# Linear attention gated by a Hadamard FFN: the second pair's transform by matrix products, a chained layernorm and a divided elu step

## The chip, the cores and the metric

The kernel runs on one core of one Trainium2 chip, and everything is computed in 32-bit floats. The metric is the device time of one execution in microseconds (us). Three runs before the change took 1621.09, 1618.7 and 1622.43 us, with a median of 1621.09 us.

## The reference, cut to what matters

The input x holds eight sequences of 512 tokens with 512 features. Every token is normalized, and the result `xn` goes two ways: into a linear attention `s`, and into a gated FFN `g` whose weights stand behind Walsh-Hadamard transforms (`fwht`). The output is `x + s * g`.

```python
xn = _layernorm(x)
q, k, v = xn @ Wq.T + bq, xn @ Wk.T + bk, xn @ Wv.T + bv
context = (elu(q) + 1) * cumsum((elu(k) + 1) * v, axis=1) * 32 ** -0.5
s = context @ Wo.T + bo
h = fwht(xn * SU_ug) / 64
up, gate = h @ W_up.T * (Ws_up * 64), h @ W_gate.T * (Ws_gate * 64)
ffn = (fwht(silu(gate) * up * SU_dp) / 64) @ W_down.T * (Wscale_dp * 64)
out = x + s * silu(ffn)
```

A transform over 512 features can be done as butterflies in nine levels of additions and subtractions, or as products with a 128x128 Hadamard matrix for seven of the levels and butterflies for the other two.

## The kernel before, in words

**Pairs.** The eight sequences are worked in four pairs, p = 0 to 3, sequences 2p and 2p+1 together. In each pair come six projections (k, v, q for two halves of the heads; `attention`, L777), then four hidden units u = 0 to 3, of which u = 0 is followed by the output projection (`project_out`, L846), and u = 1 and u = 3 by a half of the down projection (`down`, L950). In the first pair the weights are loaded raw, encoded on VectorE (`first_w`, `hidden_w`, L1010) and stored to DRAM. Later pairs stream the encoded weights back. A hidden unit of the first pair is two `gate` and two `up` groups; in later pairs it is one `hidden_unit` (L892) of seven block products.

**Products.** All products use a seven-product scheme: operands are held as seven factors P1 to P7, three or four of them sums and differences that VectorE or GpSimd makes (`outer_factors`, `inner_tokens`, `encode_tokens`, `encode_weights`). A `group` (L535) runs seven products of one projection. ScalarE copies the partial sum out of PSUM three times (`sa`, `sb`, `sc`: `snapshot`), VectorE adds the two other accumulators (`output`, L560), and the PSUM bank of `px` goes on to the next product only when the snapshot is taken.

**Order.** The program is traced by a planner. `at(place, fn)` puts a step into an agenda at a number of places ahead; one place is one product of the group. A group advances it by 14 places, a hidden unit by 49, the output projection by 28, half a down projection by 56 or a little more. The steps of a group overlap those of the next: its last products lie at places 18 and 22. `later(us, fn)` puts VectorE work into a queue that `pace` empties: behind each output, as many items as make up the given number of us, and at least one. `catch_up` empties the queue at once. `background` gives what is traced in it a priority 150 steps lower. The trace is then put into an order for each engine by priority and by what is expected to be ready, so an instruction can come well ahead of its place. Once built, each engine takes its own instructions in that order; SyncE (SP) issues nearly all DMAs.

**The tokens of the next pair.** `normalized(b)` (L179) loads sequence b, normalizes it on VectorE (statistics L202, scale L212), stores it (`put("x")`, L198), multiplies it by `su` on GpSimd (L222) and stores that too (`put("xs")`). `transformed(b)` (L244) loads this back and does nine levels of butterflies in two instructions each on VectorE (L255), then stores the result (`d_xh`). `hidden_tokens` (L297) loads it again turned around by `squares` (L262, in pieces of 128 bytes) and transposes it on VectorE (`turned`); `next_tokens` (L284) does the same with the untransformed tokens for the attention. For the first pair the transform is done differently, by `first_transform` (L348) in the attention: products with `hads`, the Hadamard matrix scaled by the signs, pinned in TensorE's program order, then two levels of butterflies.

**Where it all stands.** For the second pair (sequences 2 and 3) `normalized` is called behind groups 13 and 14 of the first pair, and `transforms(0)` behind group 16 (`plan`, L1209). For later pairs `normalized(2p + 2)` is called behind the attention, `normalized(2p + 3)` behind the output projection, and `transforms(p)` behind the second hidden unit. Tiles of sequences above 3 are in the pool `xin`, which has one buffer, shared with `squares`; the other large tiles are in `t8`, which has six.

**The rest that is touched.** `elu_plus_one` (L792) is traced as a whole behind the last product of a k or q group:

```python
for h in range(2):
    nc.scalar.activation(neg[:, h], r[:, h], AF.Relu, scale=-1.0)
    nc.scalar.activation(neg[:, h], neg[:, h], AF.Exp, scale=-1.0)
    nc.vector.scalar_tensor_tensor(r[:, h], r[:, h], 1.0, neg[:, h], ALU.add, ALU.max)
```

`chain_down` (L1194) folds the Hadamard transform into the down weights in four blocks during the first pair: ten VectorE instructions of 128x1024 each (L1036, L1041), and then four pinned products `pwd` (L1055, `fold_down`) 10 places behind them.

Of the kernel before, what the change touches and what calls it, by code (L numbers as in the profile page):

```python
# [8 lines left out]
F32 = mybir.dt.float32  # L9
# [12 lines left out]
def kernel(  # L22
# [156 lines left out]
    def normalized(b, delay=12):  # L179


        if b > 3:
            t = xin.tile([P, 3, 7, P], F32, tag="x", name=f"x_{b}").rearrange("p c s e -> p (c s e)")
            xt = t[:, : NT * D].rearrange("p (n d) -> p n d", n=NT)
            su = t[:, NT * D : (NT + 1) * D]
        else:
            xt = t8.tile([P, NT, D], F32, tag="t", name=f"x_{b}")
            su = hads
# [26 lines left out]

        def store():
            put("x")
            at(10, times_scales)

        def times_scales():  # L220
            for t in range(NT):
                nc.gpsimd.tensor_tensor(xt[:, t], xt[:, t], su, ALU.mult)  # L222
            put("xs")

        def start():
            if b > 3:
                with background():
                    for t in range(NT):
                        stats(t)
                    root()  # L230
                    for t in range(NT):
                        scaled(t)
                    store()
                return
            for t in range(NT):
                later(0.8, stats, t)
            later(0.3, root)
            for t in range(NT):
                later(0.6, scaled, t)
            later(0.0, store)  # L240

        at(delay, start)
# [19 lines left out]
    def squares(name, pool):  # L262


        if pool is t8:
# [30 lines left out]

    def hidden_tokens(b, xp):  # L297

# [46 lines left out]
        if s == 1:  # L345
            nc.vector.tensor_tensor(xo[:, P4], xo[:, P2], xo[:, P6], ALU.subtract)

    def first_transform(s, xa, xp):  # L348

        t = t8.tile([P, KD, L], F32, tag="t", name=f"xh_{s}")  # L350

        def product(c):
            x = (xa[:, (P1, P2)[c // 2]] if s == 0 else (xp[:, P7], xa[:, P3])[c // 2])[:, c % 2 : c % 2 + 3 : 2, :]
            p = ps.tile([P, 2, H], F32, tag="t", name=f"ph_{s}_{c}")
            tc.keep_in_program_order(
                nc.tensor.matmul(p, hads[:, c * P : (c + 1) * P], x, start=True, stop=True)
            )
            return p.rearrange("p a t -> p (a t)")

        def products(j):  # L360
            a, b = product(j), product(j + 2)
            nc.scalar.copy(t[:, j + 2], b)
            nc.vector.tensor_tensor(t[:, j], a, t[:, j + 2], ALU.add)
            nc.vector.tensor_tensor(t[:, j + 2], a, t[:, j + 2], ALU.subtract)

        def butterflies():
# [165 lines left out]
        return ps.tile([P, n, L // n], F32, tag=tag, bufs={"px": 3, "py": 1, "pz": 2, "t": 2}[tag], name=f"{tag}_{name}")  # L532


    def group(name, ws, rhs, dst, then, bias=(None, None)):  # L535

# [21 lines left out]
            return s  # L558

        def output(i, s, p):  # L560
            pace(nc.vector.tensor_tensor(dst[i], s, p.rearrange("p a t -> p (a t)"), ALU.add), 2.7)

        px, py, pz = (bank(t, name, 2) for t in ("px", "py", "pz"))
        sums = {}
# [212 lines left out]
    def attention(p, xo, co, get_w):  # L777
        def project(m, g, then):
# [4 lines left out]
            def whole(px):  # L783
# [8 lines left out]
        def elu_plus_one(r, name):  # L792
            neg = t8.tile([P, 2, 2, L], F32, tag="t", name=f"neg_{name}")
            for h in range(2):
                nc.scalar.activation(neg[:, h], r[:, h], AF.Relu, scale=-1.0)
                nc.scalar.activation(neg[:, h], neg[:, h], AF.Exp, scale=-1.0)
                nc.vector.scalar_tensor_tensor(r[:, h], r[:, h], 1.0, neg[:, h], ALU.add, ALU.max)

        def heads(g):
            phi = {}  # L800
# [13 lines left out]

            def with_q(q):
                k = phi["k"]
                elu_plus_one(q, f"q_{p}_{g}")
                for h in range(2):
# [3 lines left out]
                encode_tokens(nc.gpsimd, co[:, g])  # L822

            project("k", g, with_k)
            project("v", g, with_v)
# [184 lines left out]
    def hidden_w(name, src, f):  # L1010
# [13 lines left out]
    wd_f = dram.tile([FF, D], F32, tag="wd_f", name="wd_f")  # L1024

    def load_down(o):
        nc.sync.dma_start(rs[:, o % 2], wdown_t[:, o * P : (o + 1) * P].rearrange("(c p) e -> p c e", p=P))

    def butterflies_down(o, then):
# [155 lines left out]
    for c in range(KD):  # L1185
        nc.vector.tensor_scalar(hads[:, c * P : (c + 1) * P], had, col("su_ug", c), None, ALU.mult)
    groups = [0]

    def begin_down():
# [19 lines left out]
    plan = {  # L1209
        13: [lambda: normalized(2)], 14: [lambda: normalized(3)], 16: [lambda: transforms(0)],  # L1210
        0: [lambda: first_transform(0, xa, xp)], 1: [lambda: first_transform(1, xa, xp)], 2: [begin_down],
        3: [lambda: load_down(1)], 4: [lambda: nc.sync.dma_start(bo_r, bo.partition_broadcast(P))],
    }
    for n, u, j in ((16, 2, 0), (17, 2, 1), (18, 3, 0), (19, 3, 1)):
# [8 lines left out]
    def transforms(p):  # L1223

        even = transformed(2 * p + 2)
        if p:
            with background():
                for step in even[:8]:
                    step()
            even = even[8:]  # L1230
        for step in even:
            later(1.2, step)

        def odd():
# [5 lines left out]
    for p in range(B // 2):  # L1240
        more = p + 1 < B // 2
        if p:
            catch_up()
            xp = token_factors(f"xp_{p}")
            hidden_tokens(2 * p, xp)
            co = new_h(f"co_{p}")
        attention(p, xa, co, get_w)
        catch_up()
        if p and more:
            normalized(2 * p + 2)  # L1250
        hos = []
        for u in range(NU):
            if p == 0:
# [80 lines left out]
```

## Time and profile before

| what | value |
|---|---|
| median of three runs | 1621.09 us |
| the profiled execution | 1621.48 us |
| its span, first to last instruction | 1619.5 us |
| mean granted TensorE clock | 0.983 |
| TensorE busy, share of the span | 1535.8 us, 95% |
| VectorE busy | 1114.8 us, 69% |
| GpSimd busy | 479.5 us, 30% |
| ScalarE busy | 394.4 us, 24% |
| DMA, share of 16 engines | 59.1% |
| butterflies of the transforms (L255) on VectorE | 60 + 48 instructions, 77.7 + 59.1 us |

The profile names an engine (PE is TensorE, PEld its weight loads, DVE VectorE, ACT ScalarE, POOL GpSimd, SP SyncE), the line of the kernel and the tile written and read. "Idle before" is the time that an engine stood still ahead of an instruction, with what released it. A 32-bit product is two rows in the profile, one for each of two passes; passes of 512 columns follow each other every 0.43 us (four rows take 1.72 us from start to start), those of 256 columns every 0.216 us. Where the granted clock is halved, these intervals double. So one place of the planner is about 0.86 us.

### The profile page before, as it was taken

The numbers are of one execution on the slowest core, as the hardware profiler recorded it, in microseconds if no ns is written. First come the engines' busy times: TensorE is split into PE (matmuls) and PEld (weight loads), VectorE is DVE, ScalarE is ACT, GpSimd is POOL, SyncE is SP. The second block draws the span as 40 slices with busy tenths as digits, with TensorE's granted clock in tenths as the row PEclk, the third lists the DMA queues.
The fourth block names the chain that finished last, engine by engine and source line by source line (L and its number), as shares of the span: only waits on it lengthen the run. The fifth ranks groups of instructions, "written<-read, shape, count | busy, mean of one in ns | idle before, by whom it ended". The sixth has DMA issues, their size and how long they took to land. (4 is left out here: it accounts for less than half of the span.)

```text
span 1619.5 us, 15480 instructions
## 1 busy us (share of the span) xinstructions
PE 1535.8 (95%) x5792; PEld 1103.7 (68%) x5792; DVE 1114.8 (69%) x1470; ACT 394.4 (24%) x608; POOL 479.5 (30%) x270
## 2 busy tenths in 40 slices
PE   7989999897799989999999998999999999999998
PEld 3435547543484478888885476888887458888887
DVE  6999764499445984878673886598675596552673
ACT  4453221112014421111213431111211441111211
POOL 1122234142420064303611137120632026120631
PEclk9989999999899999999999999999999999999999
DMA  8347796866977256555586445737586624425462
GB/s 250 98 124 223 223 315 208 272 167 188 259 227 156 103 196 217 150 185 189 159 259 157 130 140 186 240 85 242 174 249 173 146 78 149 166 80 183 153 250 94
DMA packets 260602, 293.33 MB, mean 181 GB/s; under 512 B 107312, under 2 KB 209200, under 8 KB 256432
## 3 DMA queue, kind: packets, MB, share of 16 engines
q1 hardware_dynamic: 259856, 292.32, 59.1%
q8 instruction: 45, 0.74, 0.2%
q14 instruction: 29, 0.24, 0.0%
q10 hardware_dynamic: 672, 0.03, 0.0%
HBM read 203.72 MB, written 88.61 MB: 180 GB/s over the span
## 5 line engine op out<-in xcount | busy, mean ns | idle before, releaser
L621 PE MATMUL px_dn<-w_down,ho 128*128 128x256 f32 x1024 | 228.5, 379 | 0.0
L621 PEld LDWEIGHTS px_dn<-w_down,ho 128*128 128x128 f32 x1024 | 194.6, 190 | 28.2 <-issue 1.9
L723 PE MATMUL px_gu<-xi,w_gu 128*128 128x256 f32 x672 | 175.7, 384 | 5.0 <-DVE sb_gu L733 3.5
L723 PE MATMUL px_gu<-xp,w_gu 128*128 128x256 f32 x672 | 173.0, 380 | 1.3 <-DMA w_gu<-d_gu 1.3
L922 POOL TENSOR_TENSOR u<-u,v 128x1024 f32<-128x1024 f32 x24 | 56.1, 2360 | 350.2 <-DVE u L761 350.2
L723 PEld LDWEIGHTS px_gu<-xi,w_gu 128*128 128x128 f32 x672 | 127.3, 191 | 28.8 <-DVE sb_gu L733 4.3
L723 PEld LDWEIGHTS px_gu<-xp,w_gu 128*128 128x128 f32 x672 | 127.3, 190 | 21.0 <-DMA w_gu<-d_gu 2.0
L621 PE MATMUL pz_dn<-w_down,ho 128*128 128x256 f32 x496 | 112.9, 380 | 3.7 <-POOL ho L393 2.9
L621 PEld LDWEIGHTS pz_dn<-w_down,ho 128*128 128x128 f32 x496 | 93.5, 190 | 19.5 <-POOL ho L393 3.7
L723 PE MATMUL pz_gu<-xi,w_gu 128*128 128x256 f32 x336 | 86.6, 380 | 2.1 <-DVE a L754 1.1
L723 PE MATMUL pz_gu<-xp,w_gu 128*128 128x256 f32 x336 | 86.6, 380 | 1.1 <-DVE a L765 1.0
L967 POOL TENSOR_TENSOR s<-s,d 128x512 f32<-128x512 f32 x30 | 39.0, 1302 | 163.7 <-ACT d L966 124.6
L723 PE MATMUL py_gu<-xp,w_gu 128*128 128x256 f32 x336 | 87.4, 382 | 0.0
L390 POOL TENSOR_TENSOR co<-co 128x512 f32<-128x512 f32 x8 | 12.8, 1601 | 250.3 <-DVE co L819 250.3
L255 DVE TENSOR_TENSOR xh<-xs 128x1024 f32<-128x1024 f32 x60 | 77.7, 1325 | 7.6 <-DMA xs<-d_xs 7.2
L723 PEld LDWEIGHTS pz_gu<-xi,w_gu 128*128 128x128 f32 x336 | 63.4, 190 | 12.1 <-DVE u L754 2.0
L545 PE MATMUL px_gate<-xp,w_gate 128*128 128x512 f32 x128 | 62.7, 623 | 9.2 <-ACT sb_gate L555 9.2
L723 PEld LDWEIGHTS pz_gu<-xp,w_gu 128*128 128x128 f32 x336 | 63.7, 190 | 11.0 <-DVE a L765 2.4
L723 PEld LDWEIGHTS py_gu<-xp,w_gu 128*128 128x128 f32 x336 | 64.3, 192 | 9.3 <-DVE a L742 0.4
L621 PE MATMUL py_dn<-w_down,ho 128*128 128x256 f32 x256 | 60.4, 391 | 8.8 <-DMA w_down<-d_down 8.8
L545 PE MATMUL px_v<-xa,w_v 128*128 128x512 f32 x128 | 62.8, 611 | 6.0 <-ACT sc_v L557 6.0
L926 POOL TENSOR_TENSOR v<-v,r 128x1024 f32<-128x1024 f32 x24 | 57.4, 2410 | 24.3 <-DVE r L761 17.9
(264 smaller groups left out, 2744.6 us busy)
## 6 DMA issues: line engine op xcount, KB each, us to landing
w_gu<-d_gu SPq DMA_DIRECT2D x84, 896.0 KB, 4.5
w_down<-d_down SPq DMA_DIRECT2D x56, 512.0 KB, 3.8
d_s<-o SPq DMA_DIRECT2D x8, 1024.0 KB, 6.2
d_d<-dn SPq DMA_DIRECT2D x8, 1024.0 KB, 7.0
d<-d_d SPq DMA_DIRECT2D x8, 1024.0 KB, 6.6
s<-d_s SPq DMA_DIRECT2D x8, 1024.0 KB, 7.6
y<-in_x_dram SPq DMA_DIRECT2D x8, 1024.0 KB, 8.0
out_dram<-y SPq DMA_DIRECT2D x15, 512.0 KB, 2.8
```

Of the source, the lines that this page charges most:

```text
L255: nc.vector.tensor_tensor(y[:, :, op], x[:, :, 0], x[:, :, 1], (ALU.add, ALU.subtract)[op])
L390: eng.tensor_tensor(o[..., P5, :], o[..., P7, :], o[..., P1, :], ALU.subtract)
L545: nc.tensor.matmul(p.rearrange("p a t -> p (a t)") if len(r.shape) == 2 else p, ws[k][:, i, :], r, start=(first and k == 0), stop=(k == n ...
L621: nc.tensor.matmul(p[:, c], t[:, (2 * g + c) * P : (2 * g + c + 1) * P], ws[i](k), start=(first and k == 0 and c == cs[0]), stop=(k == n - ...
L723: nc.tensor.matmul(p[:, lane], w[:, lane, i, :], x(i), start=(first and lane == 0), stop=True, skip_group_check=True,)
L922: nc.gpsimd.tensor_tensor(r[:, m], ru1[:, m], rv[:, m], ALU.add)
L926: nc.gpsimd.tensor_tensor(rv[:, m], rv[:, m], rr[:, m], ALU.add)
L967: (nc.vector if final and (a, s) == (1, 0) else nc.gpsimd).tensor_tensor(r, r, d, ALU.mult)
```

## The change

- The butterflies of the second pair are taken out: `transforms(0)` is no longer called, and sequences 2 and 3 are not multiplied by the signs and not stored a second time. In the second pair `second_transform` stands in place of `hidden_tokens`: it rebuilds `hads` in the `xin` tile, loads sequence 3 once more by `squares`, and calls `first_transform` for both sequences, at places 8 and about 16 of the attention, followed by `inner_tokens`.
- `normalized` of the next pair's even sequence is called behind the first hidden unit, ahead of the output projection. The odd one is called 8 places behind the GpSimd multiplication of the even one, with a start 10 places later in place of 12.
- `elu_plus_one` is done in two steps, the second 5 places behind the first; the context is made in the same two steps.
- VectorE's paced work behind each output is 1.7 us in attention and 2.4 us in gate and up groups, in place of 2.7 us.
- In the first pair weights are encoded 11 places ahead in place of 7, the down blocks are folded 14 places behind their butterflies in place of 10, and a down block's chain waits until its load has been traced.

```diff
-        if b != 3:
+        if b > 3:
             nc.sync.dma_start(su, su_row.rearrange("o d -> (o d)").partition_broadcast(P))
...
             put("x")
-            at(10, times_scales)
+            if b > 3:
+                at(10, times_scales)
...
             put("xs")
+            if b % 2 == 0:
+                at(8, lambda: normalized(b + 1, 10))
...
+    def second_transform(xa, xp):
+        t = xin.tile([P, 3, 7, P], F32, tag="x", name="z_again").rearrange("p c s e -> p (c s e)")
+        z, hads = t[:, : KD * L].rearrange("p (c t) -> p c t", c=KD), t[:, KD * L : (KD + 1) * L]
+        squares("x_3", z)
+        transform_scaled(hads)
+
+        def block():
+            turned(xp, P7, z, 0)
+            later(0.0, at, 4, lambda: first_transform(3, xa, xp, hads))
+
+        at(8, lambda: first_transform(2, xa, xp, hads))
+        at(12, block)
...
+    def transform_scaled(hads):
+        for c in range(KD):
+            nc.vector.tensor_scalar(hads[:, c * P : (c + 1) * P], had, col("su_ug", c), None, ALU.mult)
...
                 outer_factors(xp, soon=True)
+                if b > 1:
+                    inner_tokens(xp)
...
-    def group(name, ws, rhs, dst, then, bias=(None, None)):
+    def group(name, ws, rhs, dst, then, bias=(None, None), time=2.4):
...
-            pace(nc.vector.tensor_tensor(dst[i], s, p.rearrange("p a t -> p (a t)"), ALU.add), 2.7)
+            pace(nc.vector.tensor_tensor(dst[i], s, p.rearrange("p a t -> p (a t)"), ALU.add), time)
...
-                (r[:, 0, 0], r[:, 1, 0], r[:, 1, 1]), whole, b,
+                (r[:, 0, 0], r[:, 1, 0], r[:, 1, 1]), whole, b, 1.7,
...
-            for h in range(2):
+
+            def half(h):
                 nc.scalar.activation(neg[:, h], r[:, h], AF.Relu, scale=-1.0)
                 nc.scalar.activation(neg[:, h], neg[:, h], AF.Exp, scale=-1.0)
                 nc.vector.scalar_tensor_tensor(r[:, h], r[:, h], 1.0, neg[:, h], ALU.add, ALU.max)
+                if then:
+                    then(h)
+
+            half(0)
+            at(5, lambda: half(1))
...
-        return w, [(7, encode)]
+        return w, [(11, encode)]
...
     def chain_down(o):
+        if o not in loaded:
+            at(4, lambda: chain_down(o))
+            return
+
...
-            at(10, folded_block)
+            at(14, folded_block)
...
-        13: [lambda: normalized(2)], 14: [lambda: normalized(3)], 16: [lambda: transforms(0)],
+        13: [lambda: normalized(2)], 14: [lambda: normalized(3)],
...
-            hidden_tokens(2 * p, xp)
+            if p == 1:
+                second_transform(xa, xp)
+            else:
+                hidden_tokens(2 * p, xp)
...
-        if p and more:
-            normalized(2 * p + 2)
...
                 hidden_unit(p, u, xp, ho, get_w, u % 2 == 1)
+                if u == 0 and more:
+                    normalized(2 * p + 2)
                 if u == 0:
                     project_out(p, co, get_w)
             hos.append(ho)
-            if p and more and u == 0:
-                normalized(2 * p + 3)
```

More of the change, by code (lines that the diff above doesn't have):

```diff
@@ L187, in normalized @@
             xt = t8.tile([P, NT, D], F32, tag="t", name=f"x_{b}")
-            su = hads
         load_x(b, xt)
-        if b != 3:
+        if b > 3:
             nc.sync.dma_start(su, su_row.rearrange("o d -> (o d)").partition_broadcast(P))
@@ L262, in squares @@
     def squares(name, pool):
-        if pool is t8:
+        if pool not in (t8, xin):
+            z = pool
+        elif pool is t8:
             z = t8.tile([P, KD, L], F32, tag="t", name=f"z_{name}")
@@ L346, in transposed, with first_transform @@
             nc.vector.tensor_tensor(xo[:, P4], xo[:, P2], xo[:, P6], ALU.subtract)
-    def first_transform(s, xa, xp):
-        t = t8.tile([P, KD, L], F32, tag="t", name=f"xh_{s}")
+    def transform_scaled(hads):
+        for c in range(KD):
+            nc.vector.tensor_scalar(hads[:, c * P : (c + 1) * P], had, col("su_ug", c), None, ALU.mult)
+    def first_transform(b, xa, xp, hads):
+        s = b % 2
+        t = t8.tile([P, KD, L], F32, tag="t", name=f"xh_{b}")
         def product(c):
             x = (xa[:, (P1, P2)[c // 2]] if s == 0 else (xp[:, P7], xa[:, P3])[c // 2])[:, c % 2 : c % 2 + 3 : 2, :]
-            p = ps.tile([P, 2, H], F32, tag="t", name=f"ph_{s}_{c}")
+            p = ps.tile([P, 2, H], F32, tag="t", name=f"ph_{b}_{c}")
             tc.keep_in_program_order(
@@ L788, in project, with elu_plus_one @@
                 f"{m}_{p}_{g}", [w[:, 0], w[:, 1]], x_rhs(xo),
-                (r[:, 0, 0], r[:, 1, 0], r[:, 1, 1]), whole, b,
+                (r[:, 0, 0], r[:, 1, 0], r[:, 1, 1]), whole, b, 1.7,
             )
-        def elu_plus_one(r, name):
+        def elu_plus_one(r, name, then=None):
             neg = t8.tile([P, 2, 2, L], F32, tag="t", name=f"neg_{name}")
-            for h in range(2):
+            def half(h):
                 nc.scalar.activation(neg[:, h], r[:, h], AF.Relu, scale=-1.0)
@@ L816, in with_q, with context @@
                 k = phi["k"]
-                elu_plus_one(q, f"q_{p}_{g}")
-                for h in range(2):
+                def context(h):
                     nc.vector.scalar_tensor_tensor(
@@ L821, in with_q @@
                     )
-                encode_tokens(nc.gpsimd, co[:, g])
+                    if h == 1:
+                        encode_tokens(nc.gpsimd, co[:, g])
+                elu_plus_one(q, f"q_{p}_{g}", context)
             project("k", g, with_k)
@@ L1019, in encode @@
                     inner_w(name, f - NU, encoded[name, f - NU], w)
-        return w, [(7, encode)]
+        return w, [(11, encode)]
     encoded = {}
     wd_f = dram.tile([FF, D], F32, tag="wd_f", name="wd_f")
+    loaded = []
     def load_down(o):
+        loaded.append(o)
         nc.sync.dma_start(rs[:, o % 2], wdown_t[:, o * P : (o + 1) * P].rearrange("(c p) e -> p c e", p=P))
@@ L1184 @@
     hads = rd[:, 2 * NF * P + D : 2 * NF * P + 2 * D]
-    for c in range(KD):
-        nc.vector.tensor_scalar(hads[:, c * P : (c + 1) * P], had, col("su_ug", c), None, ALU.mult)
+    transform_scaled(hads)
     groups = [0]
@@ L1209 @@
     plan = {
-        13: [lambda: normalized(2)], 14: [lambda: normalized(3)], 16: [lambda: transforms(0)],
-        0: [lambda: first_transform(0, xa, xp)], 1: [lambda: first_transform(1, xa, xp)], 2: [begin_down],
+        13: [lambda: normalized(2)], 14: [lambda: normalized(3)],
+        0: [lambda: first_transform(0, xa, xp, hads)], 1: [lambda: first_transform(1, xa, xp, hads)], 2: [begin_down],
         3: [lambda: load_down(1)], 4: [lambda: nc.sync.dma_start(bo_r, bo.partition_broadcast(P))],
@@ L1225, in transforms @@
         even = transformed(2 * p + 2)
[L1226 to L1231, printed above, removed]
+        with background():
+            for step in even[:8]:
+                step()
+        for step in even[8:]:
             later(1.2, step)
```

## The prediction

> **What bounds the kernel now.** I read the page first, then stretches of the span by busy time, then TensorE's waits, then VectorE's and SyncE's order in time around the largest of them.
>
> ```profile
> PE 1535.8 (95%) x5792; PEld 1103.7 (68%) x5792; DVE 1114.8 (69%) x1470; ACT 394.4 (24%) x608; POOL 479.5 (30%) x270
> ```
>
> TensorE's work sets the time. So I count what the span holds beside matmuls: a stretch loses its length less PE busy (idle), plus its length times one less the clock (slow). The columns below are stretch, length, then busy us (and instructions) of PE, weight loads, DVE, ACT, POOL; then clock, DMA share, GB/s.
>
> ```profile
> 13.00:97.00 84.00, 79.55 (x189) 35.08 (x188) 74.40 (x111) 34.80 (x55) 7.87 (x4) 0.96 0.48 147
> 97.00:180.00 83.00, 77.37 (x227) 43.68 (x226) 72.53 (x81) 35.02 (x83) 23.38 (x13) 0.96 0.67 194
> ...
> 298.00:414.00 116.00, 100.31 (x220) 43.29 (x219) 100.84 (x115) 24.46 (x36) 33.56 (x16) 0.94 0.72 213
> 414.00:483.00 69.00, 58.82 (x242) 47.28 (x241) 25.18 (x36) 6.21 (x10) 23.30 (x17) 0.93 0.92 239
> 483.00:608.00 125.00, 114.89 (x349) 66.73 (x348) 93.15 (x121) 46.76 (x59) 30.89 (x18) 0.97 0.52 150
> ...
> 863.00:940.00 77.00, 73.45 (x172) 32.66 (x171) 53.34 (x58) 30.09 (x38) 7.38 (x6) 0.98 0.51 135
> ...
> 983.00:1020.00 37.00, 30.43 (x124) 25.86 (x125) 23.22 (x35) 5.55 (x7) 19.15 (x10) 0.91 0.39 136
> ...
> 1246.00:1322.00 76.00, 72.47 (x175) 32.54 (x174) 52.37 (x55) 30.09 (x38) 8.13 (x6) 1.00 0.48 122
> ```
>
> Losses, idle + slow: 7.8 (4.45 + 3.4), 8.9 (5.6 + 3.3), 22.7 (15.7 + 7.0), 15.0 (10.2 + 4.8), 13.9 (10.1 + 3.8), 5.1, 9.9, 3.5: together 86.8 us. The stretches not shown lose 1 to 3.4 us each, and the tail is not touched. Nearly half lies in 298 to 483, the end of the first pair, where VectorE is first busy 100.84 of 116 us. TensorE's waits name the causes (engine, line, releaser: us, times, longest):
>
> ```profile
> PE px_gate L545 <- ACT sb_gate L555: 9.2, 4, 5.7
> PE py_dn L621 <- DMA w_down<-d_down: 8.8, 1, 8.8
> PE pz_gate L545 <- DVE g L561: 6.2, 2, 5.4
> PE pwd L1055 <- DVE xi L1036: 4.6, 2, 2.7
> PE px_v L545 <- ACT sc_v L557: 3.7, 1, 3.7
> ...
> PE pz_v L545 <- DVE v L561: 7.2, 3, 3.3
> PE px_o L621 <- DMA w_o<-d_o: 4.5, 1, 4.5
> PE px_gu L723 <- DVE sb_gu L733: 3.5, 2, 3.2
> ```
>
> (The first five are from the first pair, the last three from 483 to 1322.)
>
> **The transform taken from the first pair.** 36 of the 108 butterflies go (18 for each of two sequences). Two in a row take 2.35 us, so VectorE loses 36 x 1.18 = 42 us of work, all of it between 320 and 403. From 315.8 to 413 it has one gap of 1.1 us and none over 0.3; outputs queue behind butterflies, and behind the encodes that these hold up: the waits of 1.2 and 1.7 us at 359 and 364 and that of 5.4 us for `g` at 375. Without the 36, DVE is busy about 59 of 116 us. Also gone: eight GpSimd products of 1.3 us, and on SyncE 2 stores `xs`, 2 loads `xs`, 2 stores `xh`, 8 turned loads `z_xh` and one row `su`. One of these matters: SyncE stood from 281 to 287.6 ahead of the second `xs` store, which waited for GpSimd. The loads of w_gate behind it came late, VectorE's encode waited 2.09 us for them and, one weight on, 7.08 us:
>
> ```profile
> 296.19 0.42 DVE L398 TENSOR_TENSOR w_gate<-w_gate 128x256 f32<-128x256 f32 x1 [2.09 <-DMA w_gate<-in_wgate_t_dram]
> ...
> 306.57 0.42 DVE L398 TENSOR_TENSOR w_up<-w_up 128x256 f32<-128x256 f32 x1 [7.08 <-DMA w_up<-in_wup_t_dram]
> ...
> 308.05 0.68 DVE L561 TENSOR_TENSOR g<-sa_gate,py_gate 128x512 f32<-128x512 f32 x1
> ```
>
> The output `g` stands behind that encode, Silu behind `g` on ScalarE, `sb` behind Silu, and TensorE waits 5.71 us from 305, then runs slow. The change takes 6.6 us of waiting off SyncE and traces the encode 4 places (3.4 us) later; together more than the 7.08. I credit 15 of the 22.7 us (bounds: 8, about the waits for `g`, and 22.7).
>
> The 8.8 us wait for w_down at 433 is another matter: those loads were issued at 433.5, behind eight turned loads `z_x` that took SyncE from 414.0 to 431.6. 3.5 us of this was a wait for the `s_up` store to free `xin`; the rest are slow issues (up to 3.3 us, the shortest 0.57) while DMA is at 0.92. VectorE made `s_up` from 406.5 to 413, at the end of its backlog, so it comes some us earlier; the turned loads stay. I credit 5 of 15.0 (bounds 0 and 13).
>
> **The same transform in the second pair's attention.** On TensorE's path, with nothing to hide it: 8 products of two passes at 0.43 us, 6.9 us. On VectorE: `hads` 4 x 0.27, eight sums from PSUM at 0.69, four butterflies at 1.18, two transposes at 0.62, in all 12.6 us, against eight transposes (2 x 2.48 = 5.0 us) that go; and the even layernorm (4 x 0.69 + 4 x 0.54 and small ones, about 6 us) leaves this stretch. VectorE gains 1.6 us of work in 483 to 555, where it is busy 49.8 of 72. The products are pinned, so TensorE would stand if a PSUM buffer of theirs came back late; the same code at 28 to 49 in the first pair cost no wait (its `ph` rows follow at 0.43). ScalarE gets four copies of 0.59.
>
> **Attention's order.** From 530.2 to 545.7 VectorE ran twelve transposes and factor instructions with one output among them; `v` stood behind and TensorE waited 3.26 us, then ran at half clock. In pairs 2 and 3 the like cost 1.99 and about 2. With 1.7 us a step, one factor of 2.0 goes behind an output, every 4.0 us; from the places, the second pair's last comes at about 64 of 84, in time. In pairs 2 and 3 the turned loads stay as they are, and if they bunch the items, these stay bunched. The divided elu removes ScalarE's block: at 83 `sc_v` stood behind the Relu of the second half, which waited for `k`; now `sc` is traced first (place 12 against 13). That wait cost 3.67 and its slow time, and six of 0.8 in later pairs have the same releaser. In return phi is complete 4.3 us later; what needs it (v, 14 places on, and co) is not due. Credits: 6 of 7.8 in the first attention, 2 of 5.1, 2 of 3.5 (bounds: a quarter and all).
>
> **Fold and pace in the first pair.** `pwd` waited 1.90 and 2.73 us for butterflies; 4 places are 3.4 us, more than either. But at 2.4 us a step two butterflies follow an output, not three, so 40 of them need 20 outputs and not 13.3; at 4.0 us apart that is 27 us. The first half of the down weights was stored by 208.5 and read from 244.8 on; less some 13 for the store's and the load's own way, 23 us of cover. It is just used up. Credit 5 of 8.9 (bounds 0 and 8).
>
> **The layernorms.** At 583 and 981 VectorE stood 5.19 and 5.42 us for a load of x with a ready `sb_gu` behind it; TensorE lost 3.21 and, with w_o late as well, 4.50 us. These loads were late because `xin` was held by the even sequence. Now the even load finds it free, but the odd one waits as before, for GpSimd's 5.0 us and two transfers, only in a later place. I credit 8 of 13.9 in 483 to 608 (with the 3.26 above) and 5 of 9.9 in 983 to 1020. New there: L212 runs beside GpSimd, where one took 2.56 us in place of 0.53. Eight at 2 us more are 16 us of VectorE, in stretches where it idles half the time; bounds for TensorE 0 and 16, I take 6, twice the 3.3 us wait at 996.
>
> [...]
>
> **The sum.** Credits 6 + 5 + 15 + 5 + 8 + 2 + 5 + 2 = 48; debits 6.9 + 6. The span goes from 1619.5 to 1584.4. The execution's own time, 1621.48, is 1.98 more than its span: 1586.4. The median shown is 0.4 below that execution, so I say 1586.
>
> On slow time, the rows show a half-clock stretch after waits of 1.90 (at 114) and 1.99 (at 929), none after 1.58 (at 261). [...]
>
> **Rivals.**
> 1. The first pair stays bound by loads. SyncE takes 3.76 us (row at 289.74) for four of a weight's loads. If the waits at 305 and 433 stay (14.5, with 8 of slow time 22.7), 15 of the 37.7 are left to win and I would credit 10, not 20; if the later down weights add one wait like the 8.8, it is 19 less: 1605. Against: 7 MB of transfers go.
> 2. The credits hold more fully, as pair 3 shows (its attention loses 3.5, and little after): 15 more, 1571.
> 3. Slower: t8 runs short in the attentions. `neg` is held 4.3 us longer, and in pair 1 `xh_2` and `xh_3` take two of six buffers that k, v, q and two `neg` share; each time one is missing TensorE waits some 5 us with 3.4 of slow time, 8.5 us. It decides from the fifth such wait in four attentions on: 1586 + 42 = 1628. For it: all six hold d, s and y until 484. Against: the first attention held `xh_0`, `xh_1` and `r2` as well, without a wait of this kind.
> 4. That it doesn't do what it says can't well be: the call of `transforms(0)` is gone from the plan.
>
> **Numbers.** Forecast (1574 to 1597) 0.52; rival 1 (to 1617) 0.20; rival 2 (below 1574) 0.12; rival 3 0.13; no change 0.03. A measurement here tells about 0.2% from nothing. Faster is 0.52 + 0.20 + 0.12 = 0.84, same 0.03, slower 0.13. The range 1563 to 1612 leaves out the slower case, no change and a little at both ends; the bounds above lie wider on both sides, but not all will fall one way.
>
> **What would show it.** 16 `ph` rows in the second attention and no wait between them; DVE below 65 of 116 us in the last gate and up groups, without the 5.4 us wait for `g`; no 7 us wait for w_up; the w_down wait at the first pair's end at 4 to 7 us; no wait of TensorE for `sc`; L212 near the output projection at over 1 us. It is wrong if `ph` rows stand apart, if the second pair's first `xi` product waits, or if the first `px_dn` waits for w_down.

## The result, and the profile after

The changed kernel takes 1605.3 us (median of 4 runs, 1600.58 to 1607.3) beside 1620.17 us for the kernel before on the same chip: a ratio of 0.9903, 95% interval 0.9878 to 0.9928. That is faster, as forecast, but by 15 us and not by 35. The profiled execution took 1604.9 us with a span of 1603.1, 16.4 us shorter than before.

The page of the changed kernel has this line for the engines:

```profile
PE 1531.3 (96%) x5808; PEld 1102.9 (69%) x5808; DVE 1069.6 (67%) x1444; ACT 394.8 (25%) x611; POOL 461.7 (29%) x262
```

VectorE lost 45 us of work (1114.8 to 1069.6), a little more than the 42 of the butterflies, and TensorE got 16 rows more (5792 to 5808): the exchange is there. The stretches that answer to the first five of before, at the same stages (columns as there: stretch, length, busy us of PE, weight loads, DVE, ACT, POOL, then clock, DMA share, GB/s):

```profile
13.00:103.00 90.00, 84.95 (x201) 37.40 (x200) 75.56 (x108) 35.04 (x52) 11.19 (x7) 0.98 0.45 137
103.00:188.00 85.00, 70.21 (x206) 40.57 (x205) 66.91 (x82) 30.24 (x70) 21.45 (x11) 0.90 0.56 160
312.00:408.00 96.00, 93.69 (x219) 41.14 (x219) 54.41 (x82) 24.84 (x37) 26.16 (x17) 1.00 0.77 218
408.00:476.00 68.00, 62.70 (x250) 48.79 (x249) 30.87 (x43) 6.94 (x12) 20.93 (x16) 0.95 0.86 225
476.00:610.00 134.00, 130.63 (x436) 81.59 (x435) 107.40 (x139) 49.02 (x64) 50.05 (x27) 1.00 0.48 159
```

The end of the first pair (third row) is now nearly all matmuls at full clock: VectorE is busy 54.41 of 96 us, where it was 100.84 of 116. The second row went the other way: its clock fell from 0.96 to 0.90, and TensorE is idle 14.8 of 85 us where it was idle 5.6 of 83. TensorE's waits name the places (engine, line, releaser: us, times, longest):

```profile
PE px_gate L569 <- ACT sc_gate L579: 10.1, 1, 10.1
...
PE pz_gu L747 <- DVE u L778: 6.4, 3, 5.5
PE px_gate L569 <- DVE w_gate L423: 4.7, 1, 4.7
PE ph L378 <- DVE xh L386: 4.5, 1, 4.5
PE py_dn L645 <- DMA w_down<-d_down: 4.0, 1, 4.0
```

Gone are the 5.7 us for `sb_gate`, the 5.4 us for `g` and both waits of `pwd`; `w_down` fell from 8.8 to 4.0. Three waits are new, all in the first pair: `ph` at 35 us, `w_gate` at 104, `sc_gate` at 141. The wait for `u` is that of the third pair, which was forecast to go.

To compare kernels whose stages begin at different times, I take from each trace the starts of TensorE's rows, from 12 us on, cut the span at the first product of a stage, and subtract from each stretch its rows at their spacing (0.43 us, or 0.216 for 256 columns). What is left, up to the last row, is the stretch's loss, idle and slow clock together:

| loss in us | before | changed | exchange alone | first pair's pace and encode undone | best |
|---|---|---|---|---|---|
| first attention | 12.5 | 17.5 | 13.2 | 10.5 | 10.9 |
| first output projection to second gate group | 6.4 | 12.9 | 4.8 | 7.1 | 8.7 |
| second gate group and half a down projection | 4.4 | 5.7 | 4.4 | 9.0 | 4.4 |
| third and fourth gate and up groups | 22.6 | 2.9 | 3.4 | 2.7 | 3.5 |
| second half of the down projection | 13.4 | 8.7 | 2.2 | 1.8 | 1.8 |
| second pair's attention and first unit | 16.1 | 4.9 | 11.5 | 5.1 | 3.9 |
| third pair's attention to output projection | 18.2 | 15.7 | 17.9 | 18.6 | 11.8 |
| fourth attention | 4.3 | 4.0 | 6.0 | 4.0 | 4.0 |
| everything else | 9.4 | 11.8 | 11.4 | 10.4 | 8.9 |
| together | 107.0 | 84.2 | 74.7 | 69.4 | 57.8 |

(The last three columns are experiments below. The changed kernel and these three have 6.9 us more of matmul rows than before. Each column is one profiled execution, rows are rounded, and the totals were taken by themselves, so a column can miss its total by some tenths; differences of 1 us between single rows say little.) So the changed kernel wins 22.8 us of loss and pays 6.9, about the 16 us of the span. It loses 12.8 us in the first three rows, where 11 were to be won.

**What the three new waits are.** At 35 us, VectorE of the changed kernel (start, duration, line, idle time before and its releaser):

```profile
34.45 2.36 DVE L1078 TENSOR_TENSOR xi<-xi 128x1024 f32<-128x1024 f32 x2 [5.40 <-DMA xi<-in_wdown_t_dram]
36.73 0.68 DVE L585 TENSOR_TENSOR k<-sc_k,pz_k 128x512 f32<-128x512 f32 x1
```

These are the first two steps of the second down block; they stand ahead of the output `k` and wait 5.4 us for their load. `xh`, for which TensorE's `ph` waits, comes behind them. At 104 us the encode of `w_gate`, due for the next product, is mixed with the attention's scans:

```profile
105.28 0.94 DVE L422 TENSOR_TENSOR w_gate<-w_gate 128x256 f32<-128x256 f32 x1
106.14 2.33 DVE L841 TENSOR_TENSOR_SCAN k<-ones,v 128x512 f32<-128x512 f32 x2
108.39 0.39 DVE L423 TENSOR_TENSOR w_gate<-w_gate 128x256 f32<-128x256 f32 x1
```

At 141 us the chain is longer. GpSimd encodes the second block of `w_o`. Two of its instructions take 4.98 and 5.80 us; in the kernel before, this block's four took 0.72 to 0.86:

```profile
119.55 4.98 POOL L422 TENSOR_TENSOR w_o<-w_o 128x256 f32<-128x256 f32 x1 [13.62 <-DMA w_o<-in_wo_t_dram]
124.61 5.80 POOL L423 TENSOR_TENSOR w_o<-w_o 128x256 f32<-128x256 f32 x1
```

SyncE issues nothing from 117.4 to 131.80, where the store of `w_o` stands next. Behind it are the stores of `s_gate` and the next down block's load, for which VectorE then stands twice, with the ready output `g` behind:

```profile
140.88 1.09 DVE L525 TENSOR_TENSOR s_gate<-w_gate,w_gate 128x896 f32<-128x896 f32 x1 [10.46 <-DMA d_gu<-s_gate]
146.84 2.36 DVE L1078 TENSOR_TENSOR xi<-xi 128x1024 f32<-128x1024 f32 x2 [4.87 <-DMA xi<-in_wdown_t_dram]
149.12 0.68 DVE L585 TENSOR_TENSOR g<-sb_gate,pz_gate 128x512 f32<-128x512 f32 x1
```

Silu waits for `g`, `sc_gate` stands behind Silu on ScalarE, and TensorE for `sc_gate`.

### The profile page after: what moved, and what is told of

Same layout as the page of the kernel before. It is cut to its first block, busy times and chain, and to the rows that moved or that the text cites. A ratio compares the mean times of both kernels' runs of the same rounds, so it can differ in the third digit from the quotient of the medians.

```text
span 1603.1 us, 15445 instructions
## 1 busy us (share of the span) xinstructions
PE 1531.3 (96%) x5808; PEld 1102.9 (69%) x5808; DVE 1069.6 (67%) x1444; ACT 394.8 (25%) x611; POOL 461.7 (29%) x262
## 5 line engine op out<-in xcount | busy, mean ns | idle before, releaser
L414 POOL TENSOR_TENSOR co<-co 128x512 f32<-128x512 f32 x8 | 10.1, 1268 | 271.0 <-DVE co L850 271.0
L569 PE MATMUL px_gate<-xp,w_gate 128*128 128x512 f32 x128 | 63.3, 626 | 17.7 <-ACT sc_gate L579 10.1
L960 POOL TENSOR_TENSOR v<-v,r 128x1024 f32<-128x1024 f32 x24 | 58.1, 2441 | 26.4 <-DVE r L785 17.9
L569 PE MATMUL px_k<-xa,w_k 128*128 128x512 f32 x128 | 61.5, 603 | 2.0 <-ACT sc_k L581 1.6
```

Of the source, the lines that this page charges most:

```text
L414: eng.tensor_tensor(o[..., P5, :], o[..., P7, :], o[..., P1, :], ALU.subtract)
L569: nc.tensor.matmul(p.rearrange("p a t -> p (a t)") if len(r.shape) == 2 else p, ws[k][:, i, :], r, start=(first and k == 0), stop=(k == n ...
L960: nc.gpsimd.tensor_tensor(rv[:, m], rv[:, m], rr[:, m], ALU.add)
```

## Experiments

Every ratio is to the kernel before, run on the same chip; in brackets its 95% interval.

**The first pair's paced work.** My theory was that 1.7 us a step in the first attention leaves down blocks over; the rival, that the encodes at 11 places do the harm. (11 places "ahead" means later: the step is put 11 places on, so the encode is traced 4 places behind its old place.)

```diff
-                (r[:, 0, 0], r[:, 1, 0], r[:, 1, 1]), whole, b, 1.7,
+                (r[:, 0, 0], r[:, 1, 0], r[:, 1, 1]), whole, b, 1.7 if p else 2.7,
```

> The changed kernel with the attention's paced work at 2.7 us a step in the first pair and 1.7 in the others; all else as changed. Two theories of the three new waits in the first pair (4.5 us at 35, 4.7 at 104, 10.1 at 141; with slow time about 26 us). Theory A, the pace: with 1.7 us a step the first sequence's butterflies take twice as many outputs, and the second sequence's are left over and put ahead of k's outputs; with 2.7 the wait at 35 goes (6 us), and as less is pushed into the gate groups, part of the rest: 1585 to 1599 us. Theory B, the encodes 11 places ahead: the waits at 104 and 141 belong to the encodes of w_gate and w_o and stay; only the 6 us go, 1599, and none if the wait at 35 is not due to the pace.

1595.28 us, 0.9838 (0.9818 to 0.9857). The wait at 35 is gone and that of `sc_gate` is 2.0 us; `w_gate` still waits 4.1 us at 105. GpSimd's encode of that block of `w_o` lies at nearly the same place, and its instructions take 1.04 to 1.71 us:

```profile
122.77 1.04 POOL L422 TENSOR_TENSOR w_o<-w_o 128x256 f32<-128x256 f32 x1 [15.98 <-DMA d_gu<-w_gate]
```

**The encodes.**

```diff
-        return w, [(11, encode)]
+        return w, [(7, encode)]
```

> The changed kernel with the first pair's weights encoded 7 places ahead again, as before the change; all else as changed. Theory A, the pace: the waits at 35, 104 and 141 stay or go down by no more than 3 us together: 1602 to 1605 us. Theory B, the encodes: 11 places ahead puts the encode of the next weight in front of outputs that are due, and has GpSimd encode w_o while VectorE is fullest (4.98 and 5.80 us an instruction); with 7 the waits at 104 and 141 go, about 20 us: 1585, and the wait at 35 stays.

1601.71 us, 0.9868 (0.9853 to 0.9883). The wait for `w_gate` is gone and so, unexpectedly, is that of 4.0 us for `w_down` at 426: with 11 places the last `s_up` is made 4.3 us later (first instruction at 396.67 against 392.38, the stage beginning at the same time), the turned loads behind its store begin later, and `w_down`, issued behind these, goes out at 420.80 in place of 416.59. First the changed kernel, then this one:

```profile
396.67 1.08 DVE L525 TENSOR_TENSOR s_up<-w_up 128x896 f32<-128x896 f32 x1
420.80 1.04 SPq L452 DMA_DIRECT2D w_down<-d_down  x2
```

```profile
392.38 1.08 DVE L525 TENSOR_TENSOR s_up<-w_up 128x896 f32<-128x896 f32 x1
416.59 2.15 SPq L452 DMA_DIRECT2D w_down<-d_down  x2
```

The wait at 35 stays (4.3 us), and the one at 141 stays in another form: `w_o`, whose encode has a place of its own (5) that this edit leaves alone, takes GpSimd even longer, and TensorE waits 7.0 us at 156 for `g`.

```profile
113.06 7.54 POOL L422 TENSOR_TENSOR w_o<-w_o 128x256 f32<-128x256 f32 x1 [6.31 <-DMA w_o<-in_wo_t_dram]
```

**Both together.**

> The changed kernel with both: 2.7 us a step in the first pair's attention and the encodes 7 places ahead. If the two causes are separate, it wins the sum of the two: with theory A for the wait at 35 and theory B for those at 104 and 141, 26 us, 1579 us. If only one of them counts, it equals that one. If the first pair loses its time to a third thing (the fold 14 places behind, 2.4 us a step in the gate groups, the divided elu), it stays above 1597.

1592.71 us, 0.9813 (0.9798 to 0.9828), less than the 26 us I had put together. The three waits are gone (the second block of `w_o` is back at 0.72 to 0.73 us), but waits for `g` take part of the place: 7.4 us in three, one of 3.8 at 213. So the two theories divide the places between them: the pace had the waits at 35 and 141, the encodes those at 104 and 426.

**The exchange of the transform alone,** all other edits taken out:

> The kernel before with the exchange of the second pair's transform alone: paces, elu, encodes, fold and the calls of the layernorms as before (the even ones of the second pair behind groups 13 and 14 in both). By the terms of the prediction (15 and 5 us won, 6.9 spent) 1607 us. By the changed kernel's trace, where the first pair's last stretch lost 24 us less, 1602. If all of the change's gain is the transform's and its other edits cancel out, it equals the changed kernel, 1605; if the first pair's new waits come with the small edits, as theories A and B both say, they are absent here, and its first 180 us read as before.

1595.6 us, 0.9832 (0.9816 to 0.9848): the exchange alone is faster than the whole change. In the table its first three rows read as before, the fourth and fifth win 30.4 us, and the second pair wins 4.6 and pays 6.9. The other edits together cost about 10 us.

**All four small edits of the first pair undone,** to see what fold and gate pace do; and the gate pace alone put back:

```diff
-    def group(name, ws, rhs, dst, then, bias=(None, None), time=2.4):
+    def group(name, ws, rhs, dst, then, bias=(None, None), time=2.7):
...
-            at(14, folded_block)
+            at(10, folded_block)
```

> All four small edits of the first pair undone: 2.7 us a step in its attention and its gate and up groups, encodes 7 and folds 10 places ahead; the exchange of the transform, the divided elu, the layernorm calls and the pace of the later attentions stay. It stands against the kernel with only the first pair's attention pace and the encodes undone, 1592.7 us. If the fold and the pace of 2.4 us win what the prediction said (its credit 5, from waits of 1.90 and 2.73 us for the down blocks' butterflies), the waits come back: about 1597. If the pace of 2.4 us costs (that kernel waits 3.97 us for an output g at 213, and its gate groups there lose 7.0 us where the exchange alone loses 2.3), 1588. If they cancel out, 1593.

> The kernel with all four small edits of the first pair undone (ratio 0.9796), with 2.4 us a step in the gate and up groups put back. If the pace costs what the pair of fold and pace did (4.2 us by the traces, the wait for the output g at 213), 1590 us beside a before of 1621. If the fold 14 places behind did it, by pushing the products into a later place, 1588 us as without. If 2.4 wins anything alone, below 1586.

1586.4 us, 0.9796 (0.9779 to 0.9812), and 1588.15 us, 0.9789 (0.9767 to 0.9810). Only the traces tell these from the kernel with both (0.9813). With both, `pwd` waits 0.3 us and the outputs `g` 7.4; with neither, these lines:

```profile
PE pz_gate L569 <- DVE g L585: 3.8, 2, 2.4
PE px_gate L569 <- ACT sb_gate L579: 3.6, 4, 1.5
PE pz_v L569 <- DVE v L585: 3.4, 2, 1.7
PE pwd L1092 <- DVE xi L1073: 3.1, 2, 2.0
```

The waits of `pwd` do come and go with the fold as the prediction read them (the kernel with 2.4 us alone, which differs from that with both by the fold, waits 2.0 us for them); what they save is taken back at the outputs. Over the table's first three rows the kernel with 2.4 us alone loses 23.7 us, that with neither 21.8, that with both 26.6.

**The layernorm calls** at their old places, the first pair's pace and encodes undone in both:

```diff
-            if b % 2 == 0:
-                at(8, lambda: normalized(b + 1, 10))
...
-                if u == 0 and more:
-                    normalized(2 * p + 2)
...
+        if p and more:
+            normalized(2 * p + 2)
...
+            if p and more and u == 0:
+                normalized(2 * p + 3)
```

> The layernorm calls of the later pairs put back to their old places (even ones behind the attention, odd ones behind the first hidden unit); the first pair's attention pace and encodes undone in both, so it stands against 1592.7 us. By the prediction's terms (8 won in the second pair less its share of the debit for instructions beside GpSimd, 5 in the third) it is 7 to 13 us slower, 1600 to 1606. By the traces, only the second pair gains: without the new calls it loses 6.5 us at one wait near 538, and in the third pair the wait at 945 is there with either, so 6 to 7 slower, 1599. If the move does nothing, 1593.

1590.59 us, 0.9813 (0.9798 to 0.9829), the same as with the new calls. The credits for this move fall.

**The divided elu** taken out, beside the same kernel:

```diff
-            at(5, lambda: half(1))
+            half(1)
```

> Both halves of elu traced at once again; the first pair's attention pace and encodes undone in both, so it stands against 1592.7 us. By the prediction the divided step removes ScalarE's block ahead of sc of v: without it the waits of TensorE for sc_v grow (about 1 us in the first attention and 1 to 2 in each later one) and the time rises 2 to 5 us, to 1595 to 1598. Rival: the waits for sc_v follow the place of VectorE's outputs and so the pace, since with 2.7 us a step the wait near 83 is there with the divided step too (2.7 us); then it is the same, 1592 to 1594.

1601.48 us, 0.9883 (0.9868 to 0.9898): 11 us slower, which neither side expected. By the traces some 3 us more are lost up to the output projection of the first pair, 2 in the fourth attention, and 6.5 in the second pair's first hidden unit, where TensorE waits for a load of `w_gu`:

```profile
555.38 1.19 PE L747 MATMUL px_gu<-xp,w_gu 128*128 128x256 f32 x2 [4.69 <-DMA w_gu<-d_gu]
```

The kernel with the divided step runs 5.03 us earlier here and begins to issue these loads at the same distance (542.30 against 547.30 us), but waits 0.69 us. The two orders of TensorE show why: undivided, the first product of block 1, which needs the load, stands ahead of products of blocks 5 and 6, which the divided kernel runs before it.

```text
+ px_gu_0_1 <- xp, w_gu_1
+ px_gu_0_6 <- xi, w_gu_6 x2
  pz_gu_0_6 <- xp, w_gu_6 x2
+ px_gu_0_5 <- xp, w_gu_5 x2
  pz_gu_0_5 <- xi, w_gu_5 x2
+ px_gu_0_1 <- xp, w_gu_1
```

(Tiles with their block numbers; + where the order differs from the divided kernel's.)

**The later attentions' pace,** 2.7 us in all pairs, with the first pair's edits undone:

> The kernel with all four small edits of the first pair undone (ratio 0.9796), with 2.7 us a step also in the three later attentions; the divided elu stays. The prediction put part of 8 and two credits of 2 us on this pace (waits of TensorE for v behind bunched transposes and factors): then 4 to 8 us slower, 1592 to 1596 beside a before of 1621. Rival: those waits went with the divided elu, without which the later attentions lost 2 us more each and 6.6 more stood behind the second: then the same, 1587 to 1589.

1593.81 us, 0.9827 (0.9808 to 0.9845), beside 0.9796 with 1.7. The second pair's first unit loses 9.8 us in place of 2.6, at one wait of 6.3 us at 537; the attentions themselves lose the same. In this kernel, as in the exchange alone, it is the statistics of sequence 5 that stand in front. The first line below is that of the exchange alone (here they wait 7.43 us); the second is the same instruction in the kernel with divided elu, pace 1.7 and the old calls:

```profile
541.92 0.69 DVE L201 BATCH_NORM_STATS2 st<-x 128x6 f32<-128x512 f32 x1 [7.48 <-DMA x<-in_x_dram]
```

```profile
545.77 0.68 DVE L201 BATCH_NORM_STATS2 st<-x 128x6 f32<-128x512 f32 x1
```

The loads were issued at 536.63 and 538.84 us, so the load is not earlier in the second. It is VectorE that comes to it later, with other work done first. Sequence 7's wait in the third pair is the same thing, and the changed kernel has it still:

```profile
966.78 0.69 DVE L201 BATCH_NORM_STATS2 st<-x 128x6 f32<-128x512 f32 x1 [6.86 <-DMA x<-in_x_dram]
967.39 0.67 DVE L778 TENSOR_TENSOR u<-sc_gu,pz_gu 128x512 f32<-128x512 f32 x1
```

**An order edge for the odd sequence.** Its statistics may stand only behind the first output of the output projection. The order then can't lift them. (Merely tracing them 4 to 20 places later gives, in the program as built, the same order around sequence 7's first statistics as without.)

```diff
+                out = first_output.get(f"o_{b // 2 - 1}") if b % 2 else None
-                with background():
+                with background(), tc.issue_after(out.ins) if out else nullcontext():
                     for t in range(NT):
                         stats(t)
```

> The odd sequence's statistics of the later pairs may be taken on VectorE only behind the first output of the output projection (an order edge on the same engine, no wait on another); the first pair's attention pace and encodes undone in both, so it stands against 1592.7 us. Theory: the 5.5 us wait of TensorE at 945 and the half clock behind it come from the statistics of sequence 7, which stand on VectorE ahead of an output that is ready and wait 6.87 us for their load; and the 3.3 us at 963 from three scalings that take 4.86 us. Behind the output the load has landed: both go, 10 us, 1583. Rival: sequence 7 is then scaled, stored and multiplied some 15 us later, and its own transform's load or GpSimd's products for the next hidden unit take the wait over: 1590 or above.

1580.11 us, 0.9751 (0.9736 to 0.9765), from 0.9813. The wait of 5.5 us at 945 is gone, and the statistics no longer wait:

```profile
961.54 0.69 DVE L663 TENSOR_TENSOR o<-sa_o,py_o 128x512 f32<-128x512 f32 x1 [2.95 <-PE py_o L648]
962.14 1.28 DVE L203 BATCH_NORM_STATS2 st<-x 128x6 f32<-128x512 f32 x2
```

What is left there is a wait of 3.6 us for `w_o`. The takeover that the rival expected is not in the trace.

**The best of these,** the edge with all four small edits of the first pair undone, and the same with the old layernorm calls:

> Two edits put together: the first pair's paces, encode and fold places as before the change, and the odd sequence's statistics behind the output projection's first output; transform, divided elu, layernorm calls and the later attentions' pace as changed. Taken alone they brought ratios to the kernel before of 0.9796 and 0.9751, against 0.9813 with neither. If they are separate, as the places of their waits say (145 to 260 us, and 943 to 965), 0.9734: 1578 us beside a kernel before of 1621. If the order of the later part shifts with the first pair's, it stays at 0.975 or above.

> The kernel of the two edits put together, with the layernorm calls at their old places. With the statistics hindered from standing ahead of ready outputs, the place of the call could still count: by the prediction's idea the earlier start leaves more room for sequence 7's two trips through memory, and the old places are 3 to 8 us slower, 1581 to 1586. Rival, after the run with the old calls that took the same time: with the order held by data and by the one buffer, the place of the call counts for nothing, 1577 to 1579.

1578.24 us, 0.9730 (0.9711 to 0.9749), and 1576.85 us, 0.9722 (0.9700 to 0.9744). The two edits add up, and the place of the calls counts for nothing even with the edge in. Both beat the kernel before and the changed one.

**Do elu and pace win by themselves?** The edge with the exchange alone, and the best kernel with the undivided elu:

> The kernel before with the exchange of the transform alone (ratio 0.9832 without the edge) and, added to it, the order edge that keeps the odd sequence's statistics behind the output projection's first output. If pace and divided elu of the later attentions won only by where these statistics came to stand, the edge alone brings the 8 us near 537 and the 5 to 6 near 955: 0.9750, 1581 us beside a before of 1621, within 4 us of the best kernel. If they win by themselves, the waits for v and sc_v in the later attentions and the time behind them stay: 0.979 or above, 1587.

> The best kernel (ratio 0.9730, edge in place) with both halves of elu traced at once. Beside the kernel with paces and encodes undone the undivided elu cost 11 us, of it 6.6 behind the second attention, 3.4 in the first and 2 in the fourth. If the 6.6 were the statistics' place alone, 4 to 6 us remain: 0.976, 1582 us beside a before of 1621. If the divided elu frees ScalarE for the hidden unit's copies, all 11 stay: 0.980, 1588.

1584.98 us, 0.9772 (0.9752 to 0.9793), and 1587.04 us, 0.9793 (0.9774 to 0.9812). The first lies between its two forecasts: the edge brings the exchange alone 10 us. In the third pair it wins 5.2; in the second only 3.5, since a wait of 3.9 us for `w_gu` takes the place of that at 538. The second lies at its upper forecast: with the edge in, the undivided elu still costs 10 of the 11 us, 6.7 of them in the second pair, where `w_gu` waits 4.7 us with the order of TensorE shown above. So the divided elu hardly wins by where the statistics stand. The pace does: with the edge in and elu undivided, the kernel with 1.7 and the new calls (1587.04) is no faster than that with 2.7 and the old ones (1584.98). Why the order comes out so differently for so small an edit stays open.

## Why the prediction was right in sign and wrong in size

The sum by its own steps, in us won, measured as differences of loss in the table above:

| step | forecast | measured |
|---|---|---|
| attention's order in the first attention, fold and pace (6 + 5) | 11 | -12.8 |
| the transform taken from the first pair (15 + 5) | 20 | 24.4 |
| its products in the second pair | -6.9 | -6.9 |
| second pair's attention and unit, third pair's unit (8 + 5), less 6 for instructions beside GpSimd | 7 | 11.7 |
| third attention | 2 | 2.0 |
| fourth attention | 2 | 0.3 |
| stretches not touched | 0 | -2.4 |
| together (the span is 16.4 us shorter) | 35.1 | 16.3 |

- **The step that failed is "Fold and pace in the first pair", with the 6 us of the first attention.** It counted the gate groups' cover (23 us against 27) and took the later attentions' items through the places, but never those of the first attention. There 1.7 us put two items behind an output, so the first down block's last butterflies come at place 72 and the second block begins at place 82 of 84; its ten items were put in one go behind the last group, without an output ahead of them, and the order lifted the first two to 34 us. The encodes, traced 4 places later, were counted only as relief for the late loads (the 7.08 us); that `w_gate` would then come late for its own product (4.7 us at 104) was put at nothing. In place of 11 us won the runs showed 12.8 lost: the two edits undone bring the three rows from 36.1 to 26.6, all four 21.8, beside 23.3 before. With all four undone, and the edge, the kernel takes 1578, below the 1586 forecast.
- **The transform's removal** held, by its mechanism too: DVE 54.41 of 96 us, no wait for `g` at 375, none of 7 us for `w_up`. The second credit (5 of 15.0, measured 4.7) was right only by the encodes' cost: without that it is 11.2 to 11.6, near the upper bound of 13. The earlier `s_up` was worth the whole wait for `w_down`.
- **The products** cost exactly their rows, 6.9 us; there is no wait at a `ph` row in the second pair.
- **The layernorm step was wrong in its mechanism, and that its row shows 11.7 where 7 were forecast is luck.** The waits at 583 and 981 were read rightly as a load late behind a held buffer with a ready output queued behind it. But the calls do nothing: it is the order that puts the statistics there. The second pair's wait went with pace and elu (this pair loses 5 us with both, and 11.6 or 11.7 with one or neither; without the divided elu alone, at `w_gu`), the third pair's stayed (0.5 us won of 5). And the debit of 6 us didn't come. The scalings together took 20.4 us (24, mean 885 ns), against 26.3 before. The longest were one of 1.91 us at 581.87 and three in 4.86 us at 977.54; the wait of 3.6 us behind these is the old one of 3.3.
- **The divided elu** was given small credits for ScalarE's block at 83. That wait is still there with the old pace (2.7 us). The changed kernel waits 3.3 us for `sc_v` and 10.1 for `sc_gate`, so the sign "no wait of TensorE for `sc`" failed. The divided step's real worth, 11 us where it was taken out, lay for the greater part in the order of the second pair's first hidden unit. The 2 us of the third attention came as forecast, but either edit brings them nearly alone: this attention loses 6.1 us with neither, 4.4 with the pace, 4.1 with the divided elu.
- **Rival 1** gave the time of the changed kernel (1605) by luck, for another reason: the first pair did not stay bound by `w_gate`'s loads, it got new waits. **Rival 3** (the pool `t8`) is not among TensorE's waits in the trace.
- **Slow time.** The prediction took half clock to follow waits of 1.90 us, from two rows of one profile. Over all 16 profiles 28 of 57 gaps of 2 to 3 us had half clock beside or behind them, see below.

## What to carry to other kernels

A pace is a rate: lowering it spreads the queued work, so count for every stage that uses it whether the queue is still emptied by the stage's end, and what the rest is put in front of. Sequence 7's statistics, which waited 6.87 us for a load, held up TensorE for 5.5 us where the order had lifted them ahead of ready work; behind the output projection's first output they no longer waited, and the ratio went from 0.9813 to 0.9751. So bind such an instruction behind a late one of its own engine rather than call it elsewhere, and look at the orders, not at the calls. And try the parts of a change alone: here one part was worth more than the whole (1595.6 us beside 1605.3).

## What the runs showed of the hardware

**The clock.** I took the gaps between starts of TensorE's rows, less their spacing, in all 16 profiles from 20 to 1500 us. (The prediction's wait of 1.90 us is a gap of 2.06 by this count, as a matmul's row reaches 0.16 us into the next.) Of 57 gaps of 2 to 3 us, 28 touched or were followed within 4 us by half clock; of 12 from 3 to 3.5 us, 8; of 18 from 3.5 to 4 us, 16; of 28 above 4 us, all. Of 166 from 1 to 2 us it was one, inside a half-clock stretch that stood behind a gap of 2.52 us. The half-clock stretches of the changed kernel up to there last 3.4, 6.8 or 10.2 us. From 2 to 4 us half clock was beside or behind 52 of 87 gaps: there the length of a gap alone does not tell.

**GpSimd beside VectorE.** GpSimd's 128x256 additions and subtractions for `w_o` took 0.72 to 0.86 us in the kernel before, where VectorE stood idle for 1.48 us of that stretch, and 4.98, 5.80 and 7.54 us in two others (the changed kernel, and that with the encodes at 7 places) under unbroken rows of VectorE instructions. The row over the 5.80 us held 6 instructions, none above 1.21 us: one GpSimd instruction lasted as long as these together. It was not always so: with the first attention at 2.7 us, under a row as unbroken, GpSimd took 1.04 to 1.71 us and VectorE's instructions grew from 1.08 and 1.22 us to 1.61 and 1.75. What decides between the two no run here shows.
